# Tying ScalarE's scaling operations behind its PSUM copies in the last stage of a four-layer convolution kernel

## The chip, the cores and the metric

The kernel runs on one core of a Trainium2 chip. The metric is the device time of one execution in microseconds (us). The kernel before the change took 4698.92 us, the median of three runs that lay between 4698.7 and 4704.97 us.

## The reference, cut to what matters

The input is four images of 384 channels and 64 x 64 pixels in float32. Four layers are applied, each of the form `x = x + layer(groupnorm(x))`: an attention block, a feed-forward block with a Fourier filter, a block of re-weighted depthwise convolutions, and the layer that the change touches:

```
x_avg, x_max = mean and max over the pixels of the normalised x
x_w  = gelu(x_avg @ w_avg.T + b_avg + x_max @ w_max.T + b_max)      # one factor per image and channel
xr   = x_w[:, :, None] * w_mix                                      # 7 x 7 taps per image and channel
kern = gamma * (xr * Nx) + beta                                     # Nx: a norm of xr over channels
out  = x + depthwise_conv7x7(groupnorm(x), kern)
```

The 7 x 7 kernel of an image and channel is a number times the fixed taps `w_mix` plus a number times a constant 7 x 7 box. The kernel therefore computes a convolution with `w_mix` alone (the raw result, the same taps for all images), a 7 x 7 box sum, and combines `x + a * raw + b * box + offset` per image and channel.

## The kernel before

Channels are in three tiles of 128 (`j` = 0, 1, 2), images are `b` = 0 to 3, and a whole tile of one image is 128 x 4096 float32, 2 MB. The last stage is `phase_g` (L1876). It interleaves four kinds of work, each written as a Python generator that is advanced a step at a time:

- **Convolution groups**, `conv7` (L2153): 48 groups, 16 for each `j`, each of 8 channels for all images. A group has four pairs of channels and yields after each, and once more after its result is sent off: positions k = 0 to 4. A pair builds its Toeplitz block `toep` (L2169, on VectorE two times in three, else on GpSimd) and multiplies it on TensorE with the image strips in `z` (L2182). After each second pair the result `conv_m` is copied by ScalarE to `rest_o` (L2192) for `j` < 2 and sent to DRAM as `raw`; for `j` = 2 VectorE adds it to `rest_o` (L2194), which already holds the rest of the sum, and it goes out.
- **Strips**, `half_strips` (L2039): the next channels in strip layout for `z`. A piece is loaded (`strip_load`, L2024, SyncE's queue), scaled by ScalarE in place (`ax`, L2050), transposed on TensorE (L2054) and copied into `z` by ScalarE and VectorE (L2059, L2061). One piece for each group, at k = 0.
- **Last of layer three**, `x2_rest` (L2081): seven tiles of four pieces. A piece of h2 is loaded (`g_h`), scaled by ScalarE into PSUM (`x_m`, L2095), added to `x` by VectorE (L2096), squared and summed by ScalarE (L1869). 28 pieces and 7 writes make 35 steps. `factors` (L1958) then works out the numbers per channel in four advances; nothing of `raw` or `box` can be combined before it.
- **Boxes**, `boxes` (L2228): twelve tiles in the order j = 2, 0, 1, of four parts with three steps each, 144 steps. A part makes vertical sums on GpSimd and VectorE (`box_2`, `box_6`, `box_7`; in the first and last part a border row of `box_2` is filled with a constant by ScalarE, L2255), transposes them on TensorE (L2293), copies them to SBUF with ScalarE (`ht`, L2295), multiplies by a band matrix on TensorE (L2311) and adds them to `x` on VectorE (L2313). For j < 2, `after_part` (L2214) adds the raw result as well: `in_raw` is loaded at the head of the part (L2248, two buffers), scaled by ScalarE in place (L2219) and added by VectorE (L2220). It is called one part later than the part that it belongs to (`self.due`). After a tile's last part the tile is sent to DRAM by GpSimd's queue (L2224, or L2226 for j = 2).

The main loop (L1929) runs the groups, advances the strips at k = 0, and at each k advances `x2` or, once that is used up, the boxes.

This is the order in which the work is written down, the trace order. The order in an engine's queue is another[...]

PSUM tiles `x_m`, `strip_m`, `ht_m` and `box_m` share three buffers (`pm`, L365), and `conv_m` has three of its own.

Of the kernel before, what the change touches and what calls it, by code (L numbers as in the profile page):

```python
# [23 lines left out]
AF = mybir.ActivationFunctionType  # L24
# [3 lines left out]
B, C, H, W = 4, 384, 64, 64  # L28
N = H * W
NJ = 3  # L30
P = 128
# [251 lines left out]
class _Builder:  # L283
# [1592 lines left out]
    def phase_g(self):  # L1876

        tc, nc = self.tc, self.nc
        with ExitStack() as ctx:
            self.open_psum(ctx, 3)
            cp = ctx.enter_context(tc.tile_pool(name="g_const", bufs=1))
            self.gw_p = ctx.enter_context(tc.tile_pool(name="g_w", bufs=2))
            self.gt_p = ctx.enter_context(tc.tile_pool(name="g_t", bufs=2))
            self.mean384 = self.const(cp, "mean384")  # L1890
            self.band7 = self.const(cp, "band7")
            self.cols7 = self.const(cp, "cols7")

            self.band7_p = self.psum.tile([P, 512], F32, tag="band", name="band7_p", bufs=1)[:, 0:W]
            nc.vector.tensor_copy(self.band7_p, self.band7)

            for k in ("a_s", "b_s"):
                setattr(self, k, cp.tile([P, NJ, B], F32, tag=k, name=k))

            self.s_s, self.s_b = (cp.tile([P, NJ, B], F32, tag=k, name=k) for k in ("s_s", "s_b"))  # L1900
            self.a_pair = cp.tile([P, NJ, 2, 2, 2], F32, tag="a_pair", name="a_pair")

            self.gm = cp.tile([P, NJ, B], F32, tag="gm", name="gm")
            self.off = cp.tile([P, NJ, B, 3], F32, tag="off", name="off")

            self.z = self.z_[:, 0 : P * 136].rearrange("p (c k b) -> p c k b", k=34, b=B)
            self.zero = cp.tile([P, 1], F32, tag="zero", name="zero")
            nc.gpsimd.memset(self.zero, 0.0)
            self.group_means()
            self.to_strips(0, B - 1, self.x2_tile(B - 1), True)  # L1910
            for b in range(B - 1):
                self.to_strips(0, b, self.x2_tile(b))
            self.w_gate = []
            for j, (pool, tag) in enumerate(((self.gw_p, "w"), (self.gw_p, "w6"), (self.gt_p, "ht"))):
                pair = [pool.tile([P, C], F32, tag=tag, name="w_gate") for _ in range(2)]
                for t, k in zip(pair, ("w_avg_t", "w_max_t")):
                    nc.sync.dma_start(t, self.ins[k][:, j])
                self.w_gate.append(pair)
            self.pair_scales(1)

            x2 = self.x2_rest((1, 1), (1, 2), (1, 3), (2, 0), (2, 1), (2, 2), (2, 3))
            x2 = self.in_turn(x2, self.factors())
            boxes = self.all_boxes([(j, b) for j in (2, 0, 1) for b in range(B)])
            self.ready_raw = [False] * NJ
            self.mix_ahead = []
            for n in range(2):
                self.load_mix(n)
            x2_left = True
            for j in range(NJ):  # L1929
                for half in range(2):  # L1930
                    strips = self.half_strips(j + half, 1 - half) if 0 < j + half < NJ else iter(())
                    for n in range(8):
                        for k, _ in enumerate(self.conv7(j, 64 * half + 8 * n)):
                            if k == 0:
                                next(strips, None)
                            if not x2_left:
                                for _ in range(2 if k == 0 and n % 2 else 1):
                                    next(boxes, None)
                            elif k == 0 or k == 1 and n % 4 < 3:
                                x2_left = next(x2, "none") != "none"  # L1940
                    for _ in strips:
                        pass
                self.ready_raw[j] = True
            for _ in boxes:
                pass
# [93 lines left out]
    def half_strips(self, j, half):  # L2039

        nc = self.nc
        parts = [(pair, part) for pair in range(2) for part in range(3)]
        ahead = [self.strip_load(j, half, *parts[0])]
        yield
        for n, (pair, part) in enumerate(parts):
            if n + 1 < len(parts):
                ahead.append(self.strip_load(j, half, *parts[n + 1]))
            y, inside = ahead.pop(0)
            s, b = (self.a_pair[:, j, k, half, pair : pair + 1] for k in range(2))
            nc.scalar.activation(y[:, inside], y[:, inside], AF.Identity, bias=b, scale=s)  # L2050
            for i, (k0, w) in enumerate(((0, 4), (4, 4), (8, 3))):
                m = self.pm("strip_m")
                for k in range(w):
                    nc.tensor.transpose(m[:, k * P : (k + 1) * P], y[:, (k0 + k) * P : (k0 + k + 1) * P], self.ident)  # L2054
                mv = m.rearrange("p (k b c) -> p k b c", b=2, c=64)[:, 0:w]
                at = 1 + 11 * part + k0
                zv = self.z[:, 64 * half : 64 * half + 64, at : at + w, 2 * pair : 2 * pair + 2]
                if i == 1:
                    nc.vector.tensor_copy(zv.rearrange("p c k b -> p k b c"), mv)  # L2059
                else:  # L2060
                    nc.scalar.copy(zv, mv.rearrange("p k b c -> p c k b"))  # L2061
            yield
# [18 lines left out]
    def x2_rest(self, *tiles):  # L2081

        nc = self.nc
        self.x2_now, parts = {}, [(j, b, q) for j, b in tiles for q in range(4)]
        ahead = [self.x2_load(*parts[0])]
        for i, (j, b, q) in enumerate(parts):
            at = lambda v: v[:, j, b : b + 1]
            if i + 1 < len(parts):
                ahead.append(self.x2_load(*parts[i + 1]))
            h, x = ahead.pop(0), self.x2_now[j, b]  # L2090
            for v in range(2):
                m = self.pm("x2_m")
                part = slice(q * 1024 + v * 512, q * 1024 + v * 512 + 512)
                bias = at(self.g0) if j == NJ - 1 else self.zero
                nc.scalar.activation(m, h[:, v * 512 : v * 512 + 512], AF.Identity, bias=bias, scale=at(self.gh))  # L2095
                nc.vector.tensor_add(x[:, part], x[:, part], m)  # L2096
            self.x2_piece(j, b, q, x[:, q * 1024 : q * 1024 + 1024], h)
            yield
            if q == 3:
                nc.gpsimd.dma_start(self.scratch["x2"][b][j], x)  # L2100
                yield
# [51 lines left out]
    def conv7(self, j, c0):  # L2153


        nc = self.nc
# [6 lines left out]
        for pair in range(4):  # L2163
            if pair % 2 == 0:
                m = self.psum.tile([P, 512], F32, tag="c", name="conv_m", bufs=3)
# [12 lines left out]
            for c in range(2):  # L2178
                ch = 2 * pair + c
                for i in range(4):  # L2180
                    at = (c0 + ch) * 136 + 4 * i
# [7 lines left out]
            if pair % 2:  # L2189
                part = of[:, pair * 256 - 256 : pair * 256 + 256]  # L2190
                if j < NJ - 1:
                    nc.scalar.copy(part, m)  # L2192
                else:
                    nc.vector.tensor_add(part, part, m)  # L2194
            yield
# [6 lines left out]
    def all_boxes(self, tiles):  # L2202
# [8 lines left out]
            x = ahead  # L2211
        self.due()

    def after_part(self, j, b, part, x, d):  # L2214

        nc = self.nc
        if d is not None:
            xp = x[:, part * 1024 : (part + 1) * 1024]
            nc.scalar.activation(d, d, AF.Identity, bias=self.g0[:, j, b : b + 1], scale=self.a_s[:, j, b : b + 1])  # L2219
            nc.vector.tensor_add(xp, xp, d)  # L2220
        if part == 3:
            if j < NJ - 1:
                to = self.out[j].rearrange("(b m) c n -> b (m c n)", b=B)[b].rearrange("(c n) -> c n", c=P)
                nc.gpsimd.dma_start(to, x)  # L2224
            else:
                nc.gpsimd.dma_start(self.rest[:, :, b], x.rearrange("p (y n) -> p y n", n=P))  # L2226

    def boxes(self, j, b, x):  # L2228
# [3 lines left out]
        nc = self.nc  # L2232
# [4 lines left out]
        for part in range(4):  # L2237
# [7 lines left out]
            d = None  # L2245
            if j < NJ - 1:
# [5 lines left out]
            s = self.gw_p.tile([P, 10, W], F32, tag="w", name="box_2")  # L2252
            t = self.gw_p.tile([P, 8, W], F32, tag="w6", name="box_6")
            h = self.gw_p.tile([P, 16 * W], F32, tag="w7", name="box_7", bufs=3)
            fill = lambda i: nc.scalar.activation(  # L2255
                s[:, i], self.ident[:, 0:W], AF.Identity, bias=self.off[:, j, b, 2:3], scale=0.0
            )
            lo, hi = 2, 10
            if part == 0:
                fill(0)  # L2260
# [21 lines left out]
            n = 8 if part < 3 else 6  # L2282
# [6 lines left out]
            for q in range(2):  # L2289
# [2 lines left out]
                    at = (4 * q + k) * P  # L2292
                    nc.tensor.transpose(m[:, k * P : (k + 1) * P], h[:, at : at + P], self.ident)  # L2293
                ht = self.gt_p.tile([P, 512], F32, tag="ht", name="ht")
                nc.scalar.copy(ht, m)  # L2295
                if q == 0:
                    yield
                    self.box_sums(j, b, x, 2 * part, ht)
# [47 lines left out]
```

## Time and profile before

| what | time or count |
|---|---|
| median of three runs | 4698.92 us |
| profiled execution, its own time | 4707.54 us |
| its span, first to last instruction | 4705.8 us |
| last stage, first conv group to last sum | 4049.4 to 4697 us of the span |
| TensorE busy in it, granted clock | 552.6 of 647.6 us, 0.89 to 0.99 |
| VectorE, ScalarE, GpSimd busy in it | 501.6, 269.5, 348.3 us |

Times in the profile are measured from the start of the span. "Busy" leaves waits out. The granted clock is TensorE's clock as a share of full speed. A group of the profile is named by line, engine, operation, output and inputs; "idle before" is the time for which that engine stood still just ahead of these instructions, with what ended it. SPq is SyncE's queue, which issues most loads.

### The profile page before, as it was taken

The numbers are of one execution on the slowest core, as the hardware profiler recorded it, in microseconds if no ns is written. First come the engines' busy times: TensorE is split into PE (matmuls) and PEld (weight loads), VectorE is DVE, ScalarE is ACT, GpSimd is POOL, SyncE is SP. The second block draws the span as 40 slices with busy tenths as digits, with TensorE's granted clock in tenths as the row PEclk, the third lists the DMA queues.
The fourth block names the chain that finished last, engine by engine and source line by source line (L and its number), as shares of the span: only waits on it lengthen the run. The fifth ranks groups of instructions, "written<-read, shape, count | busy, mean of one in ns | idle before, by whom it ended". The sixth has DMA issues, their size and how long they took to land. (4 is left out here: it accounts for less than half of the span.)

```text
span 4705.8 us, 49802 instructions
## 1 busy us (share of the span) xinstructions
PE 4362.4 (93%) x18445; PEld 2423.8 (52%) x18445; DVE 2859.2 (61%) x4680; ACT 1992.5 (42%) x2937; POOL 807.4 (17%) x760
## 2 busy tenths in 40 slices
PE   7999999999999999998988999699999999788888
PEld 2233444344443444444548888344444444688887
DVE  7766566655566445545877788655531115767788
ACT  4444444444444444443535666311134334653332
POOL 1000000000000000000025566000000000336554
PEclk9999999999999999998989999799999999899999
DMA  4301211121111111112328999776664335895786
GB/s 144 108 33 53 93 61 68 47 75 41 54 67 61 65 34 66 56 54 82 125 90 291 321 333 332 275 264 247 252 237 172 125 140 228 296 325 165 230 277 223
DMA packets 284321, 730.36 MB, mean 155 GB/s; under 512 B 22331, under 2 KB 122790, under 8 KB 272806
## 3 DMA queue, kind: packets, MB, share of 16 engines
q1 hardware_dynamic: 213096, 407.56, 26.9%
q0 software_dynamic: 38880, 173.96, 9.8%
q10 hardware_dynamic: 32094, 145.57, 7.8%
q8 instruction: 149, 2.44, 0.2%
q14 instruction: 102, 0.84, 0.1%
HBM read 433.13 MB, written 293.86 MB: 154 GB/s over the span
## 5 line engine op out<-in xcount | busy, mean ns | idle before, releaser
L823 ACT ACTIVATE probs<-sc_s 128x1024 f32<-128x1024 f32 x512 | 496.7, 1020 | 694.0 <-PE av L933 594.3
L933 PE MATMUL av<-probs,vt 128*128 128x512 f32 x1536 | 718.7, 605 | 0.0
L1138 DVE SCALAR_TENSOR_TENSOR acc<-band,vecs,acc 128x512 f32<-128x512 f32 x708 | 496.2, 746 | 44.8 <-POOL band L1097 39.7
L1425 PE MATMUL conv_m<-toep,z 128*128 128x192 f32 (+1 forms) x2304 | 446.8, 352 | 21.7 <-DVE z L1354 11.9
L933 PEld LDWEIGHTS av<-probs,vt 128*128 128x128 f32 x1536 | 277.3, 192 | 340.6 <-issue 336.9
L1792 PE MATMUL h_m<-f_h,cm_w_t 128*128 128x512 f32 x1008 | 436.2, 595 | 7.4 <-ACT f_h L1729 7.4
L1425 PEld LDWEIGHTS conv_m<-toep,z 128*128 128x128 f32 x2304 | 402.6, 195 | 45.7 <-ACT d_o L1436 15.3
L2182 PE MATMUL conv_m<-toep,z 128*128 128x128 f32 x3072 | 388.4, 284 | 20.1 <-DVE toep L2169 16.9
L2182 PEld LDWEIGHTS conv_m<-toep,z 128*128 128x128 f32 x3072 | 375.1, 201 | 22.5 <-DVE toep L2169 17.8
L1671 PE MATMUL h_s<-e_tok,cm_w_t 128*128 128x512 f32 x768 | 362.8, 595 | 4.1 <-DMA z<-tok 4.1
L1792 PEld LDWEIGHTS h_m<-f_h,cm_w_t 128*128 128x128 f32 x1008 | 192.5, 191 | 250.7 <-issue 239.7
L815 PE MATMUL sc_s<-q,k 32*128 32x512 f32 x2048 | 306.3, 642 | 15.3 <-ACT probs L823 15.1
L1406 POOL TENSOR_TENSOR toep<-w,band 128x1280 f32<-128x1280 f32 x96 | 277.9, 2896 | 197.8 <-PE conv_m L1425 185.4
L1059 PE MATMUL t_m<-w_in_t,xb 128*128 128x384 f32 x768 | 279.8, 499 | 3.5 <-DVE coef L1076 3.4
L969 PE MATMUL proj_m<-xm,w_proj_t 128*128 128x512 f32 x576 | 269.7, 607 | 5.8 <-DVE xm L908 4.9
L1678 ACT COPY e_h<-h_s 128x1024 f32<-128x1024 f32 x96 | 97.2, 1012 | 400.4 <-PE h_s L1671 400.4
L1680 DVE BATCH_NORM_STATS2 h_st<-e_h 128x6 f32<-128x512 f32 x192 | 123.6, 685 | 219.4 <-ACT e_h L1678 219.3
L1671 PEld LDWEIGHTS h_s<-e_tok,cm_w_t 128*128 128x128 f32 x768 | 146.5, 191 | 188.5 <-issue 183.8
L976 DVE SCALAR_TENSOR_TENSOR x_res<-proj_m,bn_c,x_res 128x512 f32<-128x512 f32 x96 | 71.7, 747 | 240.3 <-PE proj_m L969 240.3
L1059 PEld LDWEIGHTS t_m<-w_in_t,xb 128*128 128x128 f32 x768 | 143.3, 192 | 141.3 <-issue 60.7
L1671 PE MATMUL h_s<-z,cm_w_t 128*128 128x512 f32 x384 | 197.0, 595 | 0.0
L838 PE MATMUL av<-probs,vt 128*32 128x512 f32 x1536 | 189.0, 604 | 4.3 <-DVE av_t L867 4.3
(464 smaller groups left out, 6353.3 us busy)
## 6 DMA issues: line engine op xcount, KB each, us to landing
d<-d_o ACTq DMA_DIRECT2D x48, 1024.0 KB
c_d<-d SPq DMA_DIRECT2D x48, 1024.0 KB
hid<-e_h ACTq DMA_DIRECT2D x16, 3072.0 KB
f_h<-hid SPq DMA_DIRECT2D x14, 3072.0 KB
x_in<-in_x SPq DMA_DIRECT2D x96, 256.0 KB
x_res<-in_x SPq DMA_DIRECT2D x32, 768.0 KB
xa<-x_res POOLq DMA_DIRECT2D x32, 768.0 KB, 3.7
xa_out<-xa SPq DMA_DIRECT2D x32, 768.0 KB
```

The source lines that it names most:

```text
L815: nc.tensor.matmul(s[:, g], lhsT=k4[32 * g : 32 * g + 32, c], rhs=q[i][32 * g : 32 * g + 32], start=True, stop=True,)
L823: nc.scalar.activation(p[:, h * 1024 : (h + 1) * 1024], s[:, 2 * h : 2 * h + 2].rearrange("p a b -> p (a b)"), AF.Exp, scale=0.25,)
L838: nc.tensor.matmul(av[k][quarter(g)], lhsT=vt[:, 4 * c + v, quarter(s)], rhs=p[:, v * 512 : (v + 1) * 512], start=c == 0 and not before, s ...
L933: nc.tensor.matmul(av[0], lhsT=vt[:, 4 * c + v, :], rhs=p[:, v * 512 : (v + 1) * 512], start=c == 0 and v == 0, stop=c == 7 and v == 3,)
L969: nc.tensor.matmul(m, lhsT=self.w_proj[:, j, o * P : (o + 1) * P], rhs=xm[:, j], start=j == 0, stop=j == NJ - 1,)
L1059: nc.tensor.matmul(m[:, 0:C], lhsT=xb[:, j], rhs=self.w_in[:, j, :], start=j == 0, stop=j == NJ - 1,)
L1138: nc.vector.scalar_tensor_tensor(out, src(j, k), w, done, ALU.mult, ALU.add)
L1406: eng.tensor_tensor(t, self.w53[:, at : at + 160].rearrange("p (m n) -> p m n", n=8).unsqueeze(2).to_broadcast([P, 20, 8, 8]), band.rearra ...
L1425: nc.tensor.matmul(m[:, c * 256 + to : c * 256 + to + 64 * (k1 - k0)], lhsT=self.z_[:, at : at + P], rhs=t[:, 10 * c + k0 : 10 * c + k1].r ...
L1671: nc.tensor.matmul(s[:, v, :], lhsT=w1[:, j, o * P : (o + 1) * P], rhs=t[j][:, v * 512 : (v + 1) * 512], start=j == 0, stop=j == NJ - 1,)
L1792: nc.tensor.matmul(m, lhsT=w2[:, o, j * P : (j + 1) * P], rhs=h[o][:, v * 512 : (v + 1) * 512], start=o == 0, stop=o == 5,)
L2182: nc.tensor.matmul(m[:, ch % 4 * P : (ch % 4 + 1) * P], lhsT=self.z_[:, at : at + P], rhs=t[:, 8 * c + 2 * i : 8 * c + 2 * i + 2].rearrang ...
```

## The change

ScalarE's scaling of strip pieces (L2050), of h2 pieces (L2095) and of raw results (L2219) is put behind the copy of ScalarE that was last written down (`rest_o` or `ht`) with `issue_after`. The border fills of the box sums go from ScalarE to GpSimd. The main loop no longer treats the factors as further `x2` steps: they are advanced at each k once `x2` is used up. The groups in which `x2` gets one step and not two are others (n = 3 and 4 of each eight, before n = 3 and 7), and boxes get a second step at k = 0 in six groups of eight, before in four.

Counted in the order written down, with groups from 0: the x2 steps end in group 20 in both; the factors took k = 0 and 1 of groups 20 and 21 and now take k = 1 to 4 of group 20; the boxes begin in group 21, at k = 0 and no longer k = 2; at the end of group 31, 63 box steps are done (before 58); the boxes are used up in group 46 at k = 0 (before in group 47 at k = 3).

```diff
@@ phase_g
-            x2 = self.in_turn(x2, self.factors())
+            factors = self.factors()
...
-            self.mix_ahead = []
+            self.mix_ahead, self.last_copy = [], None
...
-            x2_left = True
+            x2_left = factors_left = True
...
-                            if not x2_left:
-                                for _ in range(2 if k == 0 and n % 2 else 1):
+                            if x2_left:
+                                if k == 0 or k == 1 and n % 5 < 3:
+                                    x2_left = next(x2, "none") != "none"
+                            elif factors_left:
+                                factors_left = next(factors, "none") != "none"
+                            else:
+                                for _ in range(2 if k == 0 and n % 3 < 2 else 1):
                                     next(boxes, None)
-                            elif k == 0 or k == 1 and n % 4 < 3:
-                                x2_left = next(x2, "none") != "none"
@@ half_strips
-            nc.scalar.activation(y[:, inside], y[:, inside], AF.Identity, bias=b, scale=s)
+            with self.behind_copy():
+                nc.scalar.activation(y[:, inside], y[:, inside], AF.Identity, bias=b, scale=s)
@@ x2_rest
-                nc.scalar.activation(m, h[:, v * 512 : v * 512 + 512], AF.Identity, bias=bias, scale=at(self.gh))
+                with self.behind_copy():
+                    nc.scalar.activation(m, h[:, v * 512 : v * 512 + 512], AF.Identity, bias=bias, scale=at(self.gh))
@@ conv7
-                    nc.scalar.copy(part, m)
+                    self.last_copy = nc.scalar.copy(part, m)
@@
+    def behind_copy(self):
+        return self.tc.issue_after(self.last_copy.ins) if self.last_copy else nullcontext()
@@ after_part
-            nc.scalar.activation(d, d, AF.Identity, bias=self.g0[:, j, b : b + 1], scale=self.a_s[:, j, b : b + 1])
+            with self.behind_copy():
+                nc.scalar.activation(
+                    d, d, AF.Identity, bias=self.g0[:, j, b : b + 1], scale=self.a_s[:, j, b : b + 1]
+                )
@@ boxes
-            fill = lambda i: nc.scalar.activation(
-                s[:, i], self.ident[:, 0:W], AF.Identity, bias=self.off[:, j, b, 2:3], scale=0.0
-            )
+            fill = lambda i: nc.gpsimd.tensor_copy(s[:, i], self.off[:, j, b, 2:3].to_broadcast([P, W]))
...
-                nc.scalar.copy(ht, m)
+                self.last_copy = nc.scalar.copy(ht, m)
```

## The prediction

> **What bounds the kernel now.** The change touches the last stage alone. I first asked for busy times in three stretches of it: the convolution with the h2 pieces (A, to 4268 us), with the boxes of j = 2 (B, to the last raw result at 4434.5), and the sixteen groups of j = 2 with the boxes of j = 0 and 1 (C).
>
> ```profile
> 4049.40:4268.00 218.60, 186.08 (x1553) 183.31 (x1553) 153.05 (x172) 125.88 (x194) 90.62 (x73) 0.91 0.94 319
> 4268.00:4434.50 166.50, 144.13 (x1181) 141.37 (x1182) 126.81 (x165) 57.40 (x92) 108.89 (x109) 0.93 0.56 169
> 4434.50:4697.00 262.50, 222.44 (x1801) 215.22 (x1799) 221.71 (x288) 86.20 (x118) 148.79 (x135) 0.93 0.77 253
> ```
>
> Columns: length; busy time of TensorE, its weight loads, VectorE, ScalarE, GpSimd; granted clock; DMA share; GB/s. At full speed sixteen matmuls take 1.79 us in the chain that ended last, 0.112 us each, so A, B and C hold 174, 132 and 202 us of matmuls in 218.6, 166.5 and 262.5. TensorE should be the bound and is not. Next, its waits in the whole stage:
>
> ```profile
> PE box_m L2311 <- ACT ht L2295: 45.7, 20, 8.2
> PE conv_m L2182 <- DVE toep L2169: 16.9, 6, 7.7
> PE strip_m L2054 <- DVE x L2096: 8.1, 4, 3.5
> PE strip_m L2054 <- ACT ax L2050: 6.4, 1, 6.4
> PE ht_m L2293 <- ACT z L2061: 3.7, 1, 3.7
> ```
>
> The band matmul waits for ScalarE's copy `ht` (total us, times, longest), although ScalarE is busy a third of B and C. Its own waits say why: it stands before operations whose load has not landed.
>
> ```profile
> ACT in_raw L2219 <- DMA in_raw<-raw: 61.2, 25, 8.5
> ACT ax L2050 <- DMA ax<-x: 59.0, 13, 9.0
> ...
> ACT x_m L2095 <- DMA g_h<-h: 27.9, 8, 6.6
> ACT box L2255 <- DVE box_t L2272: 27.3, 13, 5.2
> ```
>
> One case in order of time, ScalarE, then TensorE just after:
>
> ```profile
> 4336.40 1.51 ACT L2050 ACTIVATE ax<-ax,a_pair 128x1344 f32<-128x1344 f32 x1 [7.63 <-DMA ax<-x]
> 4337.81 0.56 ACT L2295 COPY ht<-ht_m 128x512 f32<-128x512 f32 x1
> ```
>
> ```profile
> 4338.43 2.08 PE L2311 MATMUL box_m<-cols,ht 128*128 128x128 f32 x8 [5.28 <-ACT ht L2295]
> 4340.30 1.06 PE L2293 MATMUL ht_m<-ident,box 128*128 128x128 f32 x4
> 4341.15 2.97 PE L2182 MATMUL conv_m<-toep,z 128*128 128x128 f32 x14
> ```
>
> By the sizes of the pieces (1344, 1408, 1344, ...) this is the third of its half, whose copies into `z` run at 4358.6, over a group later; `ht` and `rest_o` copies written down before it stood behind it. The same order held TensorE for 4.36, 6.65, 8.16, 6.29 and 5.51 us (ending 4287, 4376, 4448, 4478, 4512). `in_raw` goes early too: near the end it is scaled at 4679.93 ahead of four `ht` copies that precede it in the text.
>
> [...]`ht` starts only when the waiting scaling ends. [...]after the 5.28 us stop, 8 + 4 + 14 matmuls took 2.08 + 1.06 + 2.97 us, against 1.16 + 0.60 + 1.73 undisturbed (4346.94 for the last), a loss of 2.6 us beside the stop.
>
> **The change part by part.**
>
> *Ties of `ax` and `in_raw`.* No instruction is added; 24 + 32 move back in ScalarE's queue, `ax` by up to some groups, `in_raw` by two to four `ht` copies, some 7 to 14 us. Most of their DMA waits, up to 9 us, fit inside that. What can be won: in B the three stops of 16.3 us in all, and 3 x 2.6 = 8 of slow clock; in C 29.5 us before `box_m` and the 3.7 before `ht_m` (behind an `in_raw` that waited 5.77), and 4 x 2.6 = 10. Together 24 in B and 44 in C. Not all is kept, because VectorE is next. A box part costs it 1.22 + 0.34 + 0.60 + 0.74 + 2 x 0.74 + 1.45 = 5.8 us, 1.95 a step. The faster box rate moves 5 steps (63 instead of 58 by group 31) from C to B: about 10 us. VectorE then has 137 us in B and 212 in C. Its densest stretches now are 55.25 of 60 us (4560 to 4620) and 69.06 of 77 (from 4620), 92% and 90%. At 91%, B takes 150 us and C 233. **B -16.** In C I take 236 rather than 233, for the raw loads' ring below: **C -26.** If the loads come late even at the later place, the ties win nothing, 0; if VectorE packs better, all 68.
>
> What waits behind the moved operations: for `ax`, the transposes of the piece, which TensorE now meets soon after, so that other matmuls must stand between (the piece itself is due in `z` only half a `j` later); VectorE's add L2220 for `in_raw`, then the free buffer, the next load in SyncE's queue, and all that stands behind it there (`rest_o` loads, output writes, strip and tile loads). The time 4434 to 4697 has 32 parts, 8.2 us each; after, 236/32 = 7.4. With two buffers a round is two parts, 14.8 us. It needs load (4.2 to 7.3 us from issue to scaling in the trace), 1.24 for the scaling, 1.2 to 2.2 for the add, some 2 behind copies: 9 to 13 us. That fits.
>
> *Ties of `x_m`.* 56 activations of 0.78 us go behind a `rest_o` copy; now they run one or two steps ahead. Behind them stand VectorE's add and the Toeplitz blocks; the two long stops of `conv_m` (7.67, 7.20) come that way. But A moves 319 GB/s x 218.6 us = 69.7 MB, and its best 50 us ran at 346 GB/s: 201 us are the least. The DMA is the cover and the limit: a conv that no longer stops early waits later for the same bytes. Gain at most 17; loss, if the later scaling frees the three `g_h` buffers later, up to a copy's wait of 3 us on every second of 28 pieces, 42/2 = 20. I take **A 0**, ends -17 and +20.
>
> *Fills.* ScalarE loses 24 x 0.347 = 8.3 us and 30.4 us of waits, of which only those ahead of a ready `ht` count; they are within the stops above: 0. GpSimd gains 24 small copies. No row shows a broadcast copy of 128x64; its 128x128 copies L2243 and L2263 take 0.28 undisturbed and 0.43 in the mean, so at most 24 x 0.43 = 10 us, at least 24 x 0.16 = 4 (its memset of this size). GpSimd is busy 57 to 65% and waits for the same buffer anyway (L2263 for `box_t`, 31.5 us); hidden: **0**. Without that cover, +10.
>
> *Factors in four positions of one group.* The same instructions, but about a pair of 1.8 us apart instead of some 5. Their VectorE operations with waits (2.1, 2.05, 1.04 us), two table loads of 1.28 and the activations run between matmuls in TensorE's queue. **+2**, ends 0 and +6.
>
> *The end.* Now the boxes end with the conv; the last 2 MB are issued at 4697.08 and the span ends at 4705.8; the last band matmul ended at 4694.7. Afterwards seven pairs, 7 x 1.8 = 12.6 us, follow the boxes in the text and hide this write (9.8 us median) and the last two scalings. What stays is an add of 0.7, an issue of 0.4 and the last `rest_o` write, 5.7 us in the chain: 7 instead of 11. **-4.**
>
> Sum: -16 - 26 + 0 + 0 + 2 - 4 = -44. The profiled execution took 4707.5, so 4663.5; the median of the runs is 8.6 lower: **4655 us**.
>
> **Rivals.** *The gain is half eaten* (4682, -17): `ax` and `in_raw` stay late because their loads stand in SyncE's queue behind a tile load that waits for a write (90.4 us there for `rest`, up to 45.5 at once). For it: nothing in the change frees that queue. Against: most data landed before the written place. *No change* (4699): VectorE or the DMA takes every gap; against it, VectorE idles 41 us in C. *Slower: the raw ring.* Each add now comes about a part later, the load after it, and SyncE's queue adds its own delay. At 12.5 us plus 6 of queue a round costs 18.5 instead of 14.8; over 16 rounds +59, less the 42 of B and C: 4716. It decides from a delay of 14.8 + 42/16 - 12.5 = 4.9 us on. For it: waits of up to 8.9 us before these loads now (86.3 us in 22). Against: they are waits for the very add, not for other work. [...]
>
> **From numbers to chances.** Forecast 0.60 (4632 to 4680), half 0.13, no change 0.09, slower 0.18. Leaving out the top fifth and few at the bottom: 4634 to 4705. About 0.2% (9 us) is what can be told from no change. Faster 0.73, same 0.09, slower 0.18.
>
> **What would show it.** Right: the DMA waits of L2219 and L2050 mostly gone, `box_m` waiting under 15 us for `ht`, the clock near 0.97 in B and C, VectorE at 90%, `ax` behind the group's last `ht`. Wrong: large waits of `box_m` for `ht` behind an `in_raw` that waits at its new place; A longer than 225 us; GpSimd's fills ahead of long `toep` waits.

## The result and the profile after

The changed kernel took 4653.7 us, the median of four runs between 4645.71 and 4666.46, against 4698.81 for the kernel before. The ratio is 0.9906 with an interval of 0.9879 to 0.9934. The forecast was 4655.

The profiled execution took 4666.46 us, the slowest of the four runs, 41.1 less than the one before. The last stage gained more than that: in this execution the stages ahead of it, which the change does not touch, ended later (the last h2 matmul began at 4017.8 us and not at 4008.9; the first conv group at 4058.80 and not at 4049.43). From the first conv group to the end of the span the stage took 656.4 us before and 605.9 after, 50.5 less.

For a fair comparison of the two traces I cut the stage at the raw results' writes to DRAM, which come once for each group of j < 2: A up to the write of group 20, B up to that of group 31, C up to the last sum, then the tail. The forecast had cut A from B at 4268 us, one group later; its other cuts are the same. What the later cut does to A and B stands under "B, -16" below.

| stretch | before, us | after, us | difference | forecast |
|---|---|---|---|---|
| A, conv and h2 pieces | 206.2 | 201.8 | -4.4 | 0 (-17 to +20) |
| B, conv and boxes of j = 2 | 178.9 | 161.1 | -17.8 | -16, and +2 for the factors |
| C, conv of j = 2, boxes of j = 0, 1 | 262.3 | 237.8 | -24.5 | -26 |
| tail | 9.0 | 5.2 | -3.8 | -4 |

The busy times of the changed kernel by stretch, A to C; columns as before the change: length, TensorE, its weight loads, VectorE, ScalarE, GpSimd, granted clock, DMA share, GB/s.

```profile
4058.80:4260.62 201.82, 174.75 (x1464) 173.34 (x1465) 143.10 (x159) 121.36 (x186) 81.23 (x64) 0.93 0.93 326
4260.62:4421.69 161.07, 154.81 (x1317) 152.13 (x1316) 137.47 (x188) 61.71 (x93) 127.78 (x138) 0.97 0.71 216
4421.69:4659.45 237.76, 211.95 (x1757) 204.57 (x1755) 219.72 (x276) 81.48 (x103) 143.57 (x140) 0.97 0.85 271
```

The kernel before in the same cut, B and C:

```profile
4255.59:4434.50 178.91, 155.90 (x1271) 152.75 (x1270) 134.33 (x176) 62.39 (x99) 118.30 (x118) 0.92 0.58 175
4434.50:4696.78 262.28, 222.44 (x1801) 215.22 (x1799) 221.71 (x288) 86.20 (x118) 148.79 (x135) 0.93 0.77 253
```

B and C now run at a clock of 0.97, before at 0.92 and 0.93. TensorE is busy 96% of B and VectorE 85%. In C VectorE is busy 92%, more than any other engine. TensorE's waits in the changed kernel, its whole last stage:

```profile
PE conv_m L2187 <- DVE toep L2174: 13.8, 9, 5.8
PE ht_m L2302 <- DVE box L2292: 8.3, 6, 3.3
PE box_m L2320 <- ACT ht L2304: 7.6, 7, 3.4
PE strip_m L2058 <- ACT ax L2054: 6.7, 4, 3.0
```

The wait of the band matmul for `ht` fell from 45.7 us in 20 to 7.6 in 7. What stands at the top now is VectorE. ScalarE's waits for loads in the changed kernel:

```profile
ACT x_m L2100 <- DMA g_h<-h: 28.3, 6, 8.9
...
ACT in_raw L2228 <- DMA in_raw<-raw: 19.7, 9, 5.7
...
ACT ax L2054 <- DMA ax<-x: 6.5, 3, 2.7
```

Strip pieces wait 6.5 us and not 59.0, raw results 19.7 and not 61.2. The h2 pieces wait as long as they did (27.9 before). In order of time, ScalarE of the changed kernel around a strip piece:

```profile
4339.78 0.59 ACT L2304 COPY ht<-ht_m 128x512 f32<-128x512 f32 x1 [0.74 <-PE ht_m L2302]
4340.27 1.57 ACT L2054 ACTIVATE ax<-ax,a_pair 128x1408 f32<-128x1408 f32 x1
4343.12 1.29 ACT L2065 COPY z<-strip_m 128x512 f32<-128x512 f32 x2 [1.29 <-PE strip_m L2058]
```

The piece comes behind the last `ht` of the group before (its raw write went at 4339.07), does not wait, and its copies into `z` follow within 3 us. Before, a piece stood over a group ahead of its use (scaled at 4336.40, its copies into `z` at 4358.6). The raw results moved the same way: near the end of the kernel before, `ht` copies begin at 4681.54, 4683.86, 4686.19 and 4692.09, behind the scaling at 4679.93; in the changed kernel the last two scalings begin at 4647.35, behind the last `ht` at 4646.87.

### The profile page after: what moved, and what is told of

Read it like the earlier page. It is cut to its first block, busy times and chain, and to the rows that moved or that the text cites. A ratio compares the mean times of both kernels' runs of the same rounds, so it can differ in the third digit from the quotient of the medians.

```text
span 4664.7 us, 49796 instructions
## 1 busy us (share of the span) xinstructions
PE 4356.6 (93%) x18445; PEld 2415.0 (52%) x18445; DVE 2856.1 (61%) x4680; ACT 1991.0 (43%) x2913; POOL 810.8 (17%) x784
## 4 chain that ended last, share of the span: by engine, by line
PE 70%; DVE 14%; DMA 8%; issue 3%; ACT 3%; POOL 1%; SPq 0%; ACTq 0%; DVEq 0%; POOLq 0%
PE av L933 11%; PE h_m L1792 11%; PE h_s L1671 11%; PE conv_m L1425 5%; PE sc_s L815 5%; PE proj_m L969 4%; DVE acc L1138 4%; PE t_m L1059 4%; PE conv_m L2187 3%; PE av L838 3%; PE out_m L1162 2%; PE out_m L1161 2%; PE back_m L1084 2%; DMA in_raw<-raw 2%; DMA x_in<-in_x 1%
## 5 line engine op out<-in xcount | busy, mean ns | idle before, releaser
L1425 PE MATMUL conv_m<-toep,z 128*128 128x192 f32 (+1 forms) x2304 | 446.5, 351 | 21.7 <-DVE z L1354 11.9
L2187 PE MATMUL conv_m<-toep,z 128*128 128x128 f32 x3072 | 383.7, 282 | 23.3 <-DVE toep L2174 13.8
```

Of the source, the lines that this page charges most:

```text
L1425: nc.tensor.matmul(m[:, c * 256 + to : c * 256 + to + 64 * (k1 - k0)], lhsT=self.z_[:, at : at + P], rhs=t[:, 10 * c + k0 : 10 * c + k1].r ...
L2187: nc.tensor.matmul(m[:, ch % 4 * P : (ch % 4 + 1) * P], lhsT=self.z_[:, at : at + P], rhs=t[:, 8 * c + 2 * i : 8 * c + 2 * i + 2].rearrang ...
```

## The experiments

The theory on trial: ScalarE's queue was held by scalings that stood in it too early, and the ties undo that; strip pieces held B, raw results held most of C. Rivals: the gain is the new step rates; the gain is the fills that left ScalarE. The kernel before ran along with each set; its median moved between sets (4690.1 to 4708.2, 0.4%), and two kernels that differ in the fills alone (ties_only and old_rates) came out at 0.9886 and 0.9935 in different sets, so a difference of up to some 0.5% between ratios of different sets says little. The length of the last stage leaves out the time of the earlier stages, and I use it beside the ratio; it comes from one profiled execution of each kernel.

| kernel | median, us | ratio (interval) | A | B | C | tail | last stage |
|---|---|---|---|---|---|---|---|
| before | | 1 | 206.2 | 178.9 | 262.3 | 9.0 | 656.4 |
| changed | 4653.7 | 0.9906 (0.9879 to 0.9934) | 201.8 | 161.1 | 237.8 | 5.2 | 605.9 |
| ties_only | 4654.3 | 0.9886 (0.9868 to 0.9905) | 198.9 | 160.9 | 239.1 | 9.0 | 607.8 |
| rates_only | 4680.6 | 0.9946 (0.9928 to 0.9965) | 199.2 | 178.1 | 246.5 | 3.9 | 627.8 |
| fills_only | 4693.1 | 0.9975 (0.9959 to 0.9991) | 207.2 | 174.9 | 258.3 | 9.0 | 649.4 |
| ax_tie_only | 4680.7 | 0.9949 (0.9932 to 0.9966) | 204.9 | 159.7 | 258.3 | 9.0 | 631.8 |
| raw_tie_only | 4669.8 | 0.9936 (0.9918 to 0.9954) | 202.6 | 172.9 | 239.0 | 9.1 | 623.5 |
| no_raw_tie | 4659.3 | 0.9899 (0.9872 to 0.9926) | 200.0 | 166.6 | 242.0 | 3.9 | 612.6 |
| no_ax_tie | 4678.7 | 0.9964 (0.9949 to 0.9979) | 201.1 | 181.0 | 242.5 | 5.2 | 629.8 |
| no_xm_tie | 4650.1 | 0.9917 (0.9894 to 0.9940) | 204.5 | 160.2 | 231.1 | 5.3 | 601.1 |
| act_fills | 4650.0 | 0.9905 (0.9889 to 0.9922) | 199.7 | 167.0 | 230.8 | 5.2 | 602.7 |
| old_rates | 4654.4 | 0.9935 (0.9914 to 0.9955) | 199.7 | 161.4 | 237.9 | 9.0 | 608.0 |
| pool_half | 4637.2 | 0.9856 (0.9837 to 0.9875) | 199.1 | 162.7 | 226.3 | 3.9 | 592.1 |
| pool_more | 4650.9 | 0.9880 (0.9864 to 0.9897) | 197.6 | 161.7 | 238.4 | 4.6 | 602.3 |

Stretches that do the same work differ from kernel to kernel with no cause that I could name: A lies between 197.6 and 204.9 in the kernels with a tie or the rates, and C at 237.8 in the changed kernel but at 231.1 and 230.8 in no_xm_tie and act_fills, whose C has the same convolution and box work. So less than about 7 us in A, B or C says nothing.

**One part alone.** First the three parts of the change, each put into the kernel before.

ties_only: the three `with self.behind_copy():`, the two `self.last_copy = ...` and the helper that they need, and nothing else of the diff.

> The kernel before with the three ties alone (fills on ScalarE, old rates and factors). Theory (ScalarE's queue was held by scalings that waited for their loads): -40 us, about 4659, with the waits of box_m for ht down from 45.7 to under 15. Rival rates (the gain is the boxes' faster pace and earlier end): no more than -10, about 4689. Rival fills (the gain is ScalarE freed of the fills and their waits): about 4690.

Measured: ratio 0.9886, the last stage 48.6 us shorter. TensorE's wait for `ht` and ScalarE's waits for these loads in the last stage, 45.7, 61.2 and 59.0 us before:

```profile
PE box_m L2319 <- ACT ht L2303: 12.7, 15, 1.8
ACT in_raw L2225 <- DMA in_raw<-raw: 8.4, 5, 5.2
ACT ax L2051 <- DMA ax<-x: 3.8, 2, 3.1
```

The ties alone give all that the whole change gives, but for the tail, which stays at 9.0. The theory holds, and both rivals fall as explanations of the whole. One wait grew: in A TensorE now waits 17.8 us for strip pieces (`strip_m` for `ax`, 6.4 before in the whole stage), which the prediction had said needs other matmuls in between; A is no longer for it, 198.9.

rates_only: the main loop's new conditions and the separate `factors`, with no tie and ScalarE's fills.

> The kernel before with the new step rates and the factors in one group, no ties, fills on ScalarE. Theory: -4 for the end, +2 for the factors, the stops as before: 4694 to 4700. Rival rates: -35, about 4664. Rival fills: 4699.

Measured: ratio 0.9946, 25.7 us in the medians. Neither theory nor rival had this. The tail fell to 3.9 as expected. A is 7.0 shorter, no more than the spread of A. B did not change, 178.1, although it now takes five more box steps. C fell by 15.7, to 246.5.

fills_only:

```diff
-            fill = lambda i: nc.scalar.activation(
-                s[:, i], self.ident[:, 0:W], AF.Identity, bias=self.off[:, j, b, 2:3], scale=0.0
-            )
+            fill = lambda i: nc.gpsimd.tensor_copy(s[:, i], self.off[:, j, b, 2:3].to_broadcast([P, W]))
```

> The kernel before with the border fills on GpSimd and nothing else. Theory: 0, 4694 to 4704. Rival fills: -30, about 4669, since the 30 us of waits ahead of the fills leave ScalarE's queue. Rival rates: 4699.

Measured: ratio 0.9975 (0.9959 to 0.9991), 13.3 us below the kernel before of its set (4706.4), where the theory had 0; 4 us each in B and C, within the spread. A small gain in the total where nothing else is changed; in the changed kernel none is seen (act_fills, below).

**One part left out.** Next the changed kernel with one part undone.

no_raw_tie:

```diff
-            with self.behind_copy():
-                nc.scalar.activation(d, d, AF.Identity, ...)
+            nc.scalar.activation(d, d, AF.Identity, ...)
```

> The changed kernel without the tie of the raw results' scaling. Theory: most of stretch C's gain is lost, +20 to +26 against the changed kernel, 4674 to 4680, with in_raw waiting 40 us or more for its loads again. Rivals rates and fills: within 5 us of the changed kernel, 4649 to 4659.

Measured: ratio 0.9899, 4659.3 us. The waits for the loads came back, longer in all than in the kernel before (61.2 us in 25 there), but the time did not. ScalarE of this kernel, the last stage:

```profile
ACT in_raw L2227 <- DMA in_raw<-raw: 74.9, 20, 8.2
```

C is 242.0, against 237.8 in the changed kernel and 231 in two others, with 13.8 us of `box_m` waiting for `ht` in it (29.5 in the kernel before, 7.6 in the changed one). The theory as I had written it, +20 to +26, was wrong here.

no_ax_tie:

```diff
-            with self.behind_copy():
-                nc.scalar.activation(y[:, inside], y[:, inside], AF.Identity, bias=b, scale=s)
+            nc.scalar.activation(y[:, inside], y[:, inside], AF.Identity, bias=b, scale=s)
```

> The changed kernel without the tie of the strip pieces' scaling. Theory: the stops of stretch B and those of C that came from pieces (6.29 and 5.51) return, +16 to +25 against the changed kernel, 4670 to 4679. Rivals rates and fills: within 5 us of the changed kernel, 4649 to 4659.

Measured: 4678.7 us, 25.0 above the changed kernel, as the theory had it, and 28.6 above act_fills, which ran in the same set. B is back, and so are the waits; of this kernel first stretch B, then ScalarE in the last stage:

```profile
4255.99:4436.97 180.98, 160.40 (x1317) 157.82 (x1316) 138.11 (x193) 62.27 (x94) 127.42 (x137) 0.93 0.64 192
```

```profile
ACT ax L2053 <- DMA ax<-x: 58.5, 12, 9.0
```

TensorE's waits in this B are spread otherwise than before:

```profile
PE ht_m L2301 <- ACT z L2064: 8.9, 2, 4.7
PE box_m L2319 <- ACT ht L2303: 4.3, 2, 2.5
PE box_m L2319 <- ACT z L2064: 3.5, 1, 3.5
```

All three are copies of ScalarE; `box_m` for `ht` alone was 16.3 us of B before. The clock of B is 0.93 again, against 0.95 to 0.98 in the kernels with the tie. B depends on this one tie: 159.7 to 167.0 in the nine kernels that have it, 172.9 to 181.0 in the kernel before and the four that do not.

no_xm_tie:

```diff
-                with self.behind_copy():
-                    nc.scalar.activation(m, h[:, v * 512 : v * 512 + 512], AF.Identity, bias=bias, scale=at(self.gh))
+                nc.scalar.activation(m, h[:, v * 512 : v * 512 + 512], AF.Identity, bias=bias, scale=at(self.gh))
```

> The changed kernel without the tie of the h2 pieces' scaling. Theory: stretch A is set by its transfers, so no change, 4649 to 4659. Rival (this tie gives part of the gain, by VectorE's adds no longer standing ahead of Toeplitz blocks): +8 to +15, 4662 to 4669. Rival (this tie costs, by freeing the buffers later): -5 to -10, 4644 to 4649.

Measured: 4650.1 us, A at 204.5. No difference that can be told: the tie of the h2 pieces shows no effect on the time.

act_fills: the diff of fills_only backwards, in the changed kernel.

> The changed kernel with the border fills back on ScalarE. Theory: 0 to +4, 4653 to 4658. Rival fills: +20 or more, 4674 and up.

Measured: 4650.0 us, no difference.

old_rates: the main loop of the kernel before with the ties and GpSimd's fills.

> The changed kernel with the old step rates and the factors as further x2 steps. Theory: +2 (the end +4, the factors -2), VectorE loses its earlier 10 us of boxes, so up to +10: 4654 to 4664. Rival rates: +25 or more, 4679 and up.

Measured: 4654.4 us, C 237.9, tail 9.0. With the ties in place only the tail shows what the rates are worth; C is as in the changed kernel, and 7 us above act_fills and no_xm_tie, within the spread. By its parts this kernel is ties_only with the fills moved, and the two agree in last stage (607.8 and 608.0) and median (4654.3), though not in ratio, since the kernel before ran at 4690.1 in one set and 4706.4 in the other.

**Which tie does what.** Since rates_only and no_raw_tie had shown that C yields to more than one thing, I put each of the two ties into the kernel before by itself.

> The kernel before with the tie of the strip pieces' scaling and nothing else. Theory now (pieces scaled up to three groups early are the main cause; in stretch C VectorE is the next bound, so that any one relief takes most of C's gain): B about 163 instead of 179 us, C about 247 instead of 262, some -32 in the last stage, ratio about 0.993. Rival (both ties are needed, each for its own stops): B -16, C -8 at most, the last stage -24, ratio about 0.995.

Measured: B 159.7, as expected; C 258.3, hardly changed, where I had now expected 247; the last stage 24.6 shorter and the ratio 0.9949. These are the rival's numbers: each tie is needed for its own stops.

> The kernel before with the tie of the raw results' scaling and nothing else. Theory now: B unchanged at 175 to 181, C about 248, -14 in the last stage, ratio about 0.997. Rival (the prediction's: raw results carry most of C): C 240 or less, -22 and more, ratio 0.995 or below. Rival (the tie does nothing by itself): C 258 to 263.

Measured: C 239.0, B 172.9, a little below its range. ScalarE's waits show that each tie takes away its own; ax_tie_only first, raw_tie_only second:

```profile
ACT in_raw L2223 <- DMA in_raw<-raw: 68.1, 25, 8.1
ACT ax L2051 <- DMA ax<-x: 5.3, 1, 5.3
```

```profile
ACT ax L2050 <- DMA ax<-x: 52.6, 13, 9.1
ACT in_raw L2223 <- DMA in_raw<-raw: 3.8, 3, 2.8
```

The rival written for raw_tie_only, that raw results carry most of C, was right, and my new theory, that any relief takes most of C's gain, was not: the strips' tie is no such relief.

So in the kernel before, the strips' tie takes 19.2 us from B and the raw results' tie 23.3 from C. But C's parts do not add. The raw tie alone takes 23.3, the rates alone 15.7, the two together with the rest 24.5 (31 in act_fills and no_xm_tie). Each of them makes most of the other needless: without the raw tie C is 242.0 if the rates are new, and with it C is 237.9 if they are old. With both ties C stopped between 230.8 and 239.1, as if at a floor.

**What the floor is.** VectorE is busy 92% of C. In j = 2 it builds two Toeplitz blocks in three. pool_half gives GpSimd every second block there:

```diff
-            on_pool = (c0 // 2 + pair) % 3 == 2
+            on_pool = pair % 2 == 1 if j == NJ - 1 else (c0 // 2 + pair) % 3 == 2
```

> The changed kernel with every second Toeplitz block of j = 2 on GpSimd, before every third: 32 of 64 and not about 21, so VectorE loses some 11 x 1.21 = 13 us in C and GpSimd gains 11 x 2.36 = 26. Theory (VectorE, at 93% of C, is what the ties leave as the bound): C falls by 6 to 13 us, 4641 to 4648 against 4653.7 of the changed kernel. Rival (C is held by waits for single results, not by VectorE's total): no change, 4650 to 4658. Rival (GpSimd's later blocks stop the conv): slower, 4660 and up.

Measured: C 226.3, 11.5 less than in the changed kernel and 4.5 less than in act_fills; 4637.2 us, 16.5 below the changed kernel. The changed kernel did not run in this set, and the ratio's interval, 0.9837 to 0.9875, lies below the changed kernel's but overlaps that of ties_only (from 0.9868). The last stage, 592.1, is the shortest of all, the next 601.1. So it is faster than the kernel before and most likely faster than the changed one, by an amount that is open between some 5 and 16 us.

pool_more goes on the same way, to 40 blocks of 64:

```diff
-            on_pool = (c0 // 2 + pair) % 3 == 2
+            on_pool = (pair % 2 == 1 or pair == 2 and c0 % 16 == 0) if j == NJ - 1 else (c0 // 2 + pair) % 3 == 2
```

> As pool_half, but 40 of the 64 Toeplitz blocks of j = 2 on GpSimd. VectorE was still busy 94% of C there and GpSimd 75%. Theory (VectorE's total still bounds C): 8 x 1.21 = 10 us less on VectorE, C 218 to 224, 4629 to 4635 against 4637 of pool_half. Rival (GpSimd, now at 188 of 226 us and with the box sums in the same queue, is late): C 228 or more, 4639 and up.

Measured: C 238.4 and 4650.9 us, the rival's numbers, and the gain is lost again. But it is not lost as the rival said: TensorE does not wait for GpSimd's blocks (no such wait in C). C of pool_half and then of pool_more:

```profile
4410.19:4636.49 226.30, 208.08 (x1750) 202.28 (x1750) 213.83 (x264) 81.28 (x103) 169.53 (x147) 0.98 0.88 286
```

```profile
4407.00:4645.40 238.40, 210.28 (x1757) 204.20 (x1755) 225.72 (x256) 81.53 (x103) 194.75 (x156) 0.97 0.85 271
```

VectorE has eight blocks less to do and is busy 11.9 us more, 225.72 and not 213.83, and C is 12.1 us longer, while TensorE's busy time is nearly the same. That C follows VectorE's busy time holds beyond this pair: in the seven kernels with both ties C is VectorE's busy time in C plus 12.0 to 18.0 us, in the other seven plus 22.0 to 40.6. So the floor is VectorE's time, and not the number of its blocks.

VectorE's groups in C say what made it longer; the changed kernel first, then pool_half, then pool_more (count, busy us, mean ns, idle before):

```profile
L2231 DVE TENSOR_TENSOR in_x<-in_x,in_raw 128x1024 f32<-128x1024 f32 x30 | 54.6, 1822 | 12.7 <-ACT in_raw L2228 12.6
L2174 DVE TENSOR_TENSOR toep<-wmix,band_p 128x1024 f32<-128x1024 f32 x41 | 49.3, 1207 | 0.0
...
L2281 DVE TENSOR_TENSOR box_t<-box,box 128x512 f32<-128x512 f32 x25 | 21.3, 851 | 0.1
```

```profile
L2231 DVE TENSOR_TENSOR in_x<-in_x,in_raw 128x1024 f32<-128x1024 f32 x30 | 51.5, 1715 | 10.2 <-ACT in_raw L2228 10.2
...
L2174 DVE TENSOR_TENSOR toep<-wmix,band_p 128x1024 f32<-128x1024 f32 x31 | 37.3, 1206 | 0.0
L2281 DVE TENSOR_TENSOR box_t<-box,box 128x512 f32<-128x512 f32 x25 | 30.8, 1230 | 0.4
```

```profile
L2231 DVE TENSOR_TENSOR in_x<-in_x,in_raw 128x1024 f32<-128x1024 f32 x30 | 66.2, 2208 | 6.2 <-ACT in_raw L2228 6.2
...
L2281 DVE TENSOR_TENSOR box_t<-box,box 128x512 f32<-128x512 f32 x25 | 37.0, 1479 | 0.4
L2174 DVE TENSOR_TENSOR toep<-wmix,band_p 128x1024 f32<-128x1024 f32 x23 | 27.8, 1207 | 0.6 <-PE conv_m L2187 0.6
```

From pool_half to pool_more the blocks saved 9.5 us. The two operations that read two SBUF tiles, L2231 and L2281, cost 14.7 and 6.2 more for the same count. In pool_half itself the ten blocks saved 12.0 us, and L2281 took 9.5 of them back, L2231 being 3.1 shorter. The blocks, which read their second operand from PSUM, keep 1206 ns. GpSimd is busier in pool_more, 194.75 of 238.40 us against 169.53 of 226.30. In C of the changed kernel the durations go with what GpSimd does in the same moment. The sums with no GpSimd instruction beside them took 0.68 to 0.70 us, the four that ran beside one of its Toeplitz blocks for more than half a us 1.13 to 2.36. The adds with none beside them took 1.21 to 1.23 us, the six single ones that ran beside a block for 1.6 us or more 2.70 to 3.37. VectorE's own blocks took 1.20 to 1.22 us in either case. That GpSimd's work lengthens the two operations in pool_more as well, and nothing else, is inferred; no run took that work away and left the rest. GpSimd's total does not order the durations by itself: in the twelve kernels with the old split, where GpSimd is busy 56 to 63% of C, the mean of the adds (L2231) lay between 1463 and 1822 ns and that of the sums (L2281) between 797 and 1132, and from the kernel before to the changed one the first rose while the second fell.

## Why the prediction was right

**The total.** -44 was forecast and -45.1 came in the medians, -50.5 in the last stage of the two profiled executions. Of the sum, B, C and the tail came within 2 us of their terms. Some of this closeness is luck: in act_fills and no_xm_tie C is 31 us shorter than before and not 24.5, and B's match depends on where it is cut.

**The mechanism.** Held: the queue order, not the amount of ScalarE's work, cost the time. The stops of TensorE behind `ht`, the half-speed stretch after them and the early strip pieces went as written: `box_m` under 15 us, clock 0.97, `ax` behind the group's last `ht`, VectorE at 92% of C where 90% was named. ties_only shows it by itself. In the queue of the kernel before, `ht` began at 4337.81 us, as the scaling that had waited 7.63 us for its load ended. The half speed stands in the granted clock of that kernel: 0.99 from 4300 to 4338 us, 0.52 from 4338.43, where the 5.28 us stop ended, to 4344.0, and 1.00 from there to 4350; in the first 3.5 us after each of the five other stops that the prediction lists it was 0.50. After the 5.28 us stop TensorE thus needed about 5.5 us of work to run at full speed again.

**B, -16.** Measured -17.8 with the whole change and -19.2 with the strips' tie alone, and no_ax_tie shows the cause. The size agrees only in this cut. At the write of group 21, the nearest to the forecast's 4268 us, A is 2.2 us longer than before and B 24.4 shorter; this B before, then after:

```profile
4271.32:4434.50 163.18, 141.00 (x1156) 138.22 (x1155) 123.97 (x160) 56.79 (x91) 105.64 (x107) 0.93 0.57 172
4282.90:4421.69 138.79, 134.50 (x1184) 132.25 (x1183) 124.15 (x165) 55.15 (x83) 113.63 (x123) 1.00 0.73 221
```

So B gained all of the 24 us that the forecast thought could be won, where it kept 16 because VectorE, with 137 us, would be next. That step was off. It counted all five moved steps into this B, of which two belong to group 21, before the cut. VectorE is busy 124 us here, 89%, but TensorE 134.5 us, 97%, at full clock: TensorE's own work, and not VectorE's, is what fills B now.

**C, -26.** Right in size, -24.5 to -31, and the raw results' tie by itself gives 23.3. Two steps in its working were off and partly offset each other. I gave VectorE 212 us of work in C, after moving ten to B, at 91 to 90%; it has 219.7 at 92.4%. The moved steps did leave C, but the prediction carried durations over as constants, and they were not. Before, these two groups were:

```profile
L2220 DVE TENSOR_TENSOR in_x<-in_x,in_raw 128x1024 f32<-128x1024 f32 x30 | 43.9, 1463 | 4.4 <-ACT in_raw L2219 4.2 <-issue 0.2
L2272 DVE TENSOR_TENSOR box_t<-box,box 128x512 f32<-128x512 f32 x28 | 29.0, 1037 | 0.0
```

The thirty adds of raw results grew to 54.6 us (1822 ns), and the sums `box_t` fell to 21.3 for 25 (851 ns). And the prediction booked the rates in C only as moved VectorE work beneath a cap, not as a gain of their own. rates_only shows that they are one, 15.7 us without any tie. VectorE's busy time in that C is only 2.0 us less than before. TensorE's is 10.2 us less (222.4 to 212.2), with 44 matmuls fewer and a clock of 0.97, not 0.93, and its wait for `ht` is 5.4 us less (29.5 to 24.1): the stops in C became shorter, for a reason that was not traced. The raw tie and the rates shorten the same waits for `ht`, which fits that no_raw_tie lost only 4 to 11 us in C against my +20 to +26: I had taken a term that holds in the kernel before for one that holds beside the other edits.

**The raw ring**, the mechanism of the slower rival, did not close. SyncE's waits for an add ahead of these loads fell from 86.3 us in 22 to 53.2 in 19, and the scalings at their new place wait 19.7 us.

**A, 0.** Measured -4.4, inside the ends and the spread, and no_xm_tie (204.5) shows no effect of its tie. The h2 pieces wait as long for their loads as before. That transfers set A's length agrees with 322 to 337 GB/s in all these kernels, but no run moved less data, so it is not shown.

**Fills, 0.** act_fills: no difference in the changed kernel. GpSimd's fill takes 237 ns in the median, within the bounds of 0.16 and 0.43 us. That fills_only gained 0.25%, 7 us of the last stage, was not foreseen; waits of the fills ahead of ready copies would explain it, but that is argued only.

**Factors, +2.** In the group of the boxes' start, 21, the changed kernel fell back by 6.5 us (its lead over the kernel before, from write to write, went from 4.4 to -2.2), and had it back one group later (4.1). The term's net is 0. The traces show one table load of 1.28 us there in each kernel (at 4261.13 before, at 4260.98 after), where the forecast booked two.

**The tail, -4.** Measured -3.8, and the runs split as they should: 3.9 to 5.3 in each kernel with the new rates, 9.0 or 9.1 in each with the old.

## What to carry to other kernels

When an engine that is two thirds idle holds the bound engine, read what stands in its queue just ahead of the late instruction: here scalings placed early on loads that were late held the copies behind them, TensorE waited 45.7 us for `ht`, and the ties alone made the stage 48.6 us shorter. Edits that relieve the same stretch are not to be added up; price each beside the others, against what the stretch's next engine has to do. And look at that engine's work as a share of the stretch after the edit: here the next gain, some 5 to 16 us, lay in moving about 11 of 64 blocks off VectorE, and it was gone when 8 more were moved. The stretch can also change its next engine: after the same ties it was TensorE in B and VectorE in C.

## What the runs showed of the hardware

The duration of a VectorE add of two SBUF tiles of 128x1024 was no constant: 1463 ns in the mean before, 1822 in the changed kernel, 2208 in pool_more, where GpSimd was busiest, with single ones from 1202 to 7547. A multiply of the same size with one operand in PSUM stayed between 1206 and 1209 in all of them. Before more work is moved to GpSimd in such a stretch, it pays to watch these adds: in pool_more they cost VectorE more than the moved blocks saved.

After a stop of 5.28 us TensorE took 6.11 us for 26 matmuls that took 3.49 undisturbed, in the kernel before. The granted clock was 0.52 in that time and 1.00 in the 6 us behind it. In this case the stop cost half as much again, 2.6 us, after it had ended.
